# Two tiles of attention output go back to tokens together

## The chip, the cores and the metric

One core of one Trainium2 chip runs the whole program in one launch. The metric is device time in microseconds (us). Before the change three runs took 2543.44, 2546.03 and 2556.37 us; the median is 2546.03 us.

Five engines work side by side and each takes its instructions in the order in which they were built: TensorE (PE, its weight loads shown apart as PEld), VectorE (DVE), ScalarE (ACT), GpSimd (POOL) and SyncE (SP), which here only issues transfers. Results of PE land in PSUM, where this program has two kinds of tiles, banks of 512 columns and pairs of 1024.

## The reference, cut to what matters

Eight sequences of 256 tokens, 128 features each, pass through four blocks. Each block adds an attention to a given context and then an FFN, both behind a layer norm and both scaled by a gate:

```python
x = x + jnp.tanh(g_xattn[n]) * xattn_n(_layernorm(x), ctx_1024, ...)
x = x + jnp.tanh(g_ffn[n]) * ffn_n(_layernorm(x), ...)
```

The blocks differ. Block 0 has a linear attention, and its "FFN" is a self-attention of 16 heads of 8 features plus eight linear experts. Block 1 keeps the 64 largest scores of each row (8 heads of 64). Block 2 is a plain attention of 16 heads of 8, block 3 the same with the 32 largest scores of each row kept. Their output projection is

```python
qh, kh, vh = proj(q, Wq, bq), proj(k, Wk, bk), proj(v, Wv, bv)
attn = softmax(einsum('bhqd,bhkd->bhqk', qh, kh) / sqrt(8))
out = einsum('bhqk,bhkd->bhqd', attn, vh).transpose(0, 2, 1, 3).reshape(B, S, 128)
return einsum('bsd,ed->bse', out, Wo) + bo
```

The FFNs of blocks 1 to 3 are mixtures of 8, 8 and 16 experts; that of block 3 has the experts' projections around an attention of one head.

## The kernel before

**Tiling.** The 2048 tokens stay on the chip in four groups (`NG`), each a tile `xs[g]` of 128 partitions by 4 token tiles by 128 features. A group holds two batches (sequences, `bb`) of 256 tokens, so a batch is two token tiles, numbered `2 * bb + qc`.

**Way back of an attention output.** Attention with small heads leaves its output transposed: features of four heads, padded to 32 rows each, on the partitions, tokens along the columns, in two tiles `oTs` of a batch. `heads_back` (L336) turns it back. For each of the two token tiles it transposes four 128x128 pieces into a bank `pn` (L341), takes the reciprocals of the softmax sums, which lie in column 8 of each head (L345), multiplies and writes the 128 features of the tile to a tile `o_sb` of the ring `out2` (L347), and passes it to `done`. There are two sorts of `done`. Block 0's FFN adds the tile to the residual at once, with `add_gated` (L1081, L290). Blocks 2 and 3 run `out_proj` (L320): transpose `o_sb` into a bank `pt_o` (L324), copy it with ACT to `oT` (L326), multiply it by the output weights into a bank `po` (L330), add the bias by a further matmul (L333), and add the bank to the residual with `add_gated`. `out_proj` had an argument for several chunks of features, which is 1 in both uses. Block 1 has its own way back (L1229) and calls `add_gated` too.

Banks are a ring of 4, pairs a ring of 2, `out2` a ring of 6: a new tile waits until the tile that had its place is no longer used.

**Order of the work.** The program is written by Python generators, which yield between small steps. Two streams of them are interleaved by `side_by_side` (L72), by a time that each reports. One, `largest_scores` (L1683), holds the attentions of blocks 1 and 3, whose search for the largest scores is done on DVE with MAX8 and MATCH_REPLACE8 (`largest`, L385 and L389, block 3) or on ACT, POOL and DVE by counting (block 1). The other, `others` (L1799), holds all other stages, in the order of the list at L1793. A stage of one stream may start only when a set says that the other stream has got there: `finished` (called `largest_3` outside) gets a group in block 3's `finish` (L1394) after the group's last `heads_back`, and block 3's FFN of group `g` may start when `g` is in it, that of group 0 when group 2 is as well (L1763).

Behind a body, the rest of the stage before (`heads_back`, wrapped in `Ahead` with a number of steps: 6 in `attention_T.body`, 12 for block 3's `weigh` that ends in `finish`) is taken step by step as the body goes on. In the attentions with largest scores the unit is a chunk `k` of four heads: `units` searches chunk `k`, calls `fetch(k + 1)` for the next one's scores (L420, L427) when three of its four heads are through, and beside it the chunk before is weighed.

The generators only fix the order in which the program is written. Within it a scheduler of the framework, with a timeline of its own, orders the instructions of each engine.

Of the kernel before, what the change touches and what calls it, by code (L numbers as in the profile page):

```python
# [14 lines left out]
ALU = mybir.AluOpType  # L15
AX = mybir.AxisListType

P = 128
D = 128
B = 8  # L20
S = 256
# [69 lines left out]
def gated_blocks_kernel(ctx: ExitStack, tc: tile.TileContext, a, out):  # L91
    nc = tc.nc
# [8 lines left out]
    def program(exact):  # L101


        def cst(shape, name, dt=F32):
            return const.tile(shape, dt, tag=name, name=name)
# [4 lines left out]
        def bank(name="bank"):  # L110
            return psum.tile([P, 512], F32, tag="bank", name=name, bufs=4)
# [8 lines left out]
        def out2(name):  # L120
            return act.tile([P, 512], F32, tag="out2", name=name, bufs=6)
# [5 lines left out]
        xs = []  # L127
# [23 lines left out]
        ident = cst([P, P], "ident")  # L151
# [3 lines left out]
        biases = cst([P, D], "biases")  # L155
# [67 lines left out]
        tgx = cst([P, 4], "tgx")  # L223
        tgf = cst([P, 4], "tgf")
# [36 lines left out]
        def layer_norm(g):  # L261

            xg = xs[g]
            st = small.tile([P, NT, 6], F32, tag="st", name="st", bufs=2)
            mv = small.tile([P, NT, 2], F32, tag="mv", name="mv", bufs=2)
            for t in range(NT):
                nc.vector.bn_stats(st[:, t, :], xg[:, t, :])
                nc.vector.bn_aggr(mv[:, t, :], st[:, t, :])
            ve = small.tile([P, NT], F32, tag="ve", name="ve")
            nc.vector.tensor_scalar_add(ve, mv[:, :, 1], LN_EPS)  # L270
            rstd = small.tile([P, NT], F32, tag="rstd", name="rstd")
            nc.gpsimd.tensor_tensor(rstd, ve, neg_half[:, 0:NT], ALU.pow)
            xn = act.tile([P, NT, D], F32, tag="xn", name="xn", bufs=2)
            for t in range(NT):
                nc.vector.tensor_scalar(
                    xn[:, t, :], xg[:, t, :], mv[:, t, 0:1], rstd[:, t : t + 1], ALU.subtract, ALU.mult
                )
            yield
            yield
            pt = bank("pt_ln")  # L280
            for t in range(NT):
                nc.tensor.transpose(pt[:, t * P : (t + 1) * P], xn[:, t, :], ident)
            xnT = act.tile([P, W], F32, tag="xnT", name="xnT", bufs=3)
            nc.scalar.copy(xnT, pt)
            yield
            return xn, xnT

        def add_gated(g, t, src, gate):

            nc.vector.scalar_tensor_tensor(xs[g][:, t, :], src, gate, xs[g][:, t, :], ALU.mult, ALU.add)  # L290

        def heads_T(w, src, bias, scale, tag):

            dst = act.tile([P, 4, S], F32, tag=tag, name=tag, bufs=2)
            for cp in range(2):
                pp = bank("pp").rearrange("p (c q) -> p c q", c=2)
                for j in range(2):
                    c = 2 * cp + j
                    nc.tensor.matmul(pp[:, j, :], lhsT=w[:, c * P : (c + 1) * P], rhs=src, start=True, stop=True)  # L299
                if bias is None:  # L300
                    nc.scalar.mul(dst[:, 2 * cp : 2 * cp + 2, :], pp, scale)
                else:
                    for j in range(2):
                        c = 2 * cp + j
                        nc.scalar.activation(dst[:, c, :], pp[:, j, :], AF.Identity, bias=bias[:, c : c + 1], scale=scale)
            return dst

        def values16(w, srcT, width, tag):

            va = act.tile([P, 2, 16, width], F32, tag=tag, name="va", bufs=2)  # L310
            if width > 9:
                nc.gpsimd.memset(va[:, :, :, 8:width], 0.0)
            nc.gpsimd.memset(va[:, :, :, 8:9], 1.0)
            pp = bank("pv")[:, 0:256].rearrange("p (t d) -> p t d", t=2)
            for t in range(2):
                nc.tensor.matmul(pp[:, t, :], lhsT=srcT[:, t * P : (t + 1) * P], rhs=w, start=True, stop=True)
            nc.scalar.copy(va[:, :, :, 0:8], pp.rearrange("p t (h d) -> p t h d", d=8))
            return va

        def out_proj(g, t, o_sb, chunks, w, bias, gate):  # L320

            pt = bank("pt_o")
            for c in range(chunks):
                nc.tensor.transpose(pt[:, c * P : (c + 1) * P], o_sb[:, c * P : (c + 1) * P], ident)  # L324
            oT = out2("oT")
            nc.scalar.copy(oT[:, 0 : chunks * P], pt[:, 0 : chunks * P])  # L326
            yield
            po = bank("po")
            for c in range(chunks):
                nc.tensor.matmul(  # L330
                    po[:, 0:D], lhsT=oT[:, c * P : (c + 1) * P], rhs=w[:, c, :], start=(c == 0), stop=False
                )
            nc.tensor.matmul(po[:, 0:D], lhsT=bias, rhs=biases, start=False, stop=True)  # L333
            add_gated(g, t, po[:, 0:D], gate)

        def heads_back(g, bb, oTs, done):  # L336

            for qc in range(2):
                pn = bank("pn").rearrange("p (c r d) -> p c r d", c=4, r=4)
                for c in range(4):  # L340
                    nc.tensor.transpose(  # L341
                        pn[:, c].rearrange("p r d -> p (r d)"), oTs[c // 2][:, c % 2, qc * P : (qc + 1) * P], ident
                    )
                rec = small.tile([P, 4, 4], F32, tag="rec", name="rec")
                nc.vector.reciprocal(rec, pn[:, :, :, 8])  # L345
                o_sb = out2("o_sb")[:, 0:D].rearrange("p (c r d) -> p c r d", c=4, r=4)
                nc.vector.tensor_tensor(  # L347
                    o_sb, pn[:, :, :, 0:8], rec.unsqueeze(3).to_broadcast([P, 4, 4, 8]), ALU.mult
                )
                yield  # L350
                yield from done(g, 2 * bb + qc, o_sb.rearrange("p c r d -> p (c r d)"))

        def chunk_products(o, va, c, es):

# [312 lines left out]
        class attention_T:  # L667
# [5 lines left out]
            def __init__(self, g, prepare, done):  # L673
                self.g, self.prepare, self.done = g, prepare, done
# [71 lines left out]
            def body(self, first):  # L746

                behind = Ahead(0, iter(()))
                second = Ahead(11, self.ready(1))
                for bb, operands in ((0, first), (1, None)):  # L750
                    oTs = []
                    others = [behind]
                    if bb == 0:
                        others.append(second)
                    else:
                        operands = second.finish()
                    for f in alongside(self.weigh(*operands, oTs), *others):
                        yield (bb + f) / 2
                    behind = Ahead(6, heads_back(self.g, bb, oTs, self.done))
                return behind  # L760
# [118 lines left out]
        for g in range(NG):  # L879
            pt = bank("pt_c")  # L880
# [5 lines left out]
            for t in range(NT):  # L886
                n = g * NT + t
# [190 lines left out]

        class block0_ffn:
            def __init__(self, g):  # L1080
                def done(g, t, o):  # L1081
                    add_gated(g, t, o, tgf[:, 0:1])
                    yield

                self.g, self.att = g, attention_T(g, self.operands, done)
# [256 lines left out]
        def context_operands(n, weights, k=""):  # L1342
            wq, wk, wv, wo, bq, bk, bo = weights
            norms = {}

            def prepare(g, bb):
                if g not in norms:
                    norms[g] = yield from layer_norm(g)
                xnT = norms[g][1][:, bb * S : (bb + 1) * S]
                cT = ctxT[:, g * W + bb * S : g * W + (bb + 1) * S]  # L1350
                kT = heads_T(wk, cT, bk, 1.0, "kT" + k)
                yield
                qT = heads_T(wq, xnT, bq, INV_SQRT8, "qT" + k)
                yield
                return qT, kT, values16(wv, cT, 32, "va" + k)

            def done(g, t, o):
                yield from out_proj(g, t, o, 1, wo.unsqueeze(1), bo, tgx[:, n : n + 1])
                yield

            return prepare, done
# [6 lines left out]
        def block3_xattn(groups, weights, rounds, room, dropped, may_start, finished):  # L1368
# [25 lines left out]
            def finish(i, g, bb):  # L1394
                yield from heads_back(g, bb, oTs.pop(i), done)
                if bb == 1:
                    finished.add(g)
# [490 lines left out]
```

## Time and profile before

| what | value |
|---|---|
| median of three runs | 2546.03 us |
| the profiled execution | 2546.42 us, its span 2544.7 us |
| busy PE, PEld | 2123.7 us (83%), 1292.4 us (51%) |
| busy DVE, ACT, POOL | 1762.5 us (69%), 1149.0 us (45%), 879.8 us (35%) |
| granted TensorE clock, mean | 0.862 |
| MAX8 of block 3's search (L385) | 326.8 us, x768 from `wk`, 426 ns each |
| DMA | 13 GB/s in the mean |

The span reaches from the first to the last instruction. A busy share is an average over stages with different limits: block 1's search runs from about 150 to 1150 us, block 3's from 1192 to 2347 us, and block 3's FFN fills the rest to 2538 us. A row of a group shows line, engine, operation, output and input tile, shapes, count, then busy time and mean ns of one, then idle time before it with what ended most of it. A row of the timeline shows start, duration, engine, line, operation, and in brackets the idle time just before and its releaser.

### The profile page before, as it was taken

The page shows a single profiled execution, that of the slowest core. Times are in us where ns is not written, and L with a number is a line of the kernel's source. Part 1 is how long each engine was busy: PE and PEld are TensorE (multiplying, and loading weights), DVE is VectorE, ACT ScalarE, POOL GpSimd, SP SyncE. Part 2 cuts the span into 40 slices and gives each one's busy share as a digit, 9 for nine tenths or more (in the row PEclk, how much of TensorE's full clock was granted, in tenths as well). Part 3 has the DMA queues.
Part 4 walks back from the last instruction along what each step waited for, and adds up shares of the span by engine and source line. Part 5 has one row for each costly group of instructions (what it writes and reads, how often), then busy time and mean ns, then how long its engine had stood idle before and what let it go on. Part 6 is the DMA issues. An engine that isn't in the chain of part 4 may idle for free.

```text
span 2544.7 us, 35734 instructions
## 1 busy us (share of the span) xinstructions
PE 2123.7 (83%) x12068; PEld 1292.4 (51%) x12094; DVE 1762.5 (69%) x5463; ACT 1149.0 (45%) x2437; POOL 879.8 (35%) x2252
## 2 busy tenths in 40 slices
PE   7998888887878778888989868899676975988898
PEld 5655455554445444445444435445343444666677
DVE  4635757756765667665899879894798869798332
ACT  2236556546554677864355433464333542322101
POOL 3104434434432464531334324341233334233000
PEclk8999889978988889998599966899775986999999
DMA  2000001000000000010001100021000110000000
GB/s 63 6 1 2 1 1 32 1 1 1 1 1 1 1 26 1 26 34 22 1 1 42 34 1 1 1 59 50 1 1 1 42 42 1 1 5 1 5 5 6
DMA packets 47896, 32.97 MB, mean 13 GB/s; under 512 B 4747, under 2 KB 42838, under 8 KB 47702
## 3 DMA queue, kind: packets, MB, share of 16 engines
q1 hardware_dynamic: 47702, 30.58, 4.2%
q8 instruction: 97, 1.59, 0.3%
q14 instruction: 97, 0.79, 0.1%
HBM read 29.53 MB, written 1.05 MB: 12 GB/s over the span
## 4 chain that ended last, share of the span: by engine, by line
DVE 39%; PE 36%; ACT 13%; POOL 8%; issue 4%; DMA 0%; DVEq 0%; SPq 0%; ACTq 0%; POOLq 0%
DVE m L385 13%; DVE wk L389 12%; ACT signs L495 4%; PE sm L687 3%; PE sw L723 3%; PE ph L1476 3%; PE pp L299 3%; PE y L1445 2%; DVE nmz L695 2%; PE po L1635 2%; ACT sign L495 2%; PE oT L357 2%; PE o L1216 2%; DVE xe L851 2%; DVE list L542 1%
## 5 line engine op out<-in xcount | busy, mean ns | idle before, releaser
L392 POOL TENSOR_SCALAR mask<-rooms,m 128x256 bf16<-128x256 f32 x192 | 223.3, 1163 | 385.5 <-DVE m L385 353.4
L385 DVE MAX8 m<-wk 128x8 f32<-128x256 f32 x768 | 326.8, 426 | 37.0 <-DVE wk L389 0.9
L723 PE MATMUL sw<-qT,kT 32*128 32x256 f32 x1024 | 172.4, 476 | 68.3 <-ACT eK L599 24.1
L695 DVE TENSOR_REDUCE nmz<-sm 128x4 f32<-128x1024 f32 x128 | 154.9, 1219 | 105.1 <-PE sm L687 96.6
L389 DVE MATCH_REPLACE8 wk<-m,wk 128x256 f32<-128x256 f32 x512 | 208.9, 408 | 0.0
L495 ACT ACTIVATE signs<-room,nt 128x256 bf16<-128x256 f32 x288 | 145.9, 507 | 128.7 <-POOL nt L527 78.5
L687 PE MATMUL sm<-kT,qT 32*128 32x256 f32 x1024 | 152.6, 440 | 40.0 <-DVE nmz L695 28.4
L592 ACT ACTIVATE kept<-mask 128x1024 bf16<-128x1024 bf16 x64 | 67.6, 1057 | 227.3 <-POOL mask L392 227.1
L1476 PE MATMUL ph<-xnT,we 128*128 128x512 f32 x288 | 156.2, 638 | 15.5 <-ACT hT L1477 7.4
L723 PEld LDWEIGHTS sw<-qT,kT 32*128 32x128 f32 x1024 | 101.0, 222 | 128.4 <-DVE nmz L695 32.3
L737 ACT ACTIVATE eT<-sw 128x1024 f32<-128x1024 f32 x128 | 129.6, 1019 | 79.9 <-PE sw L723 73.9
L574 PE MATMUL sw<-qTk,kTk 32*128 32x256 f32 (+1 forms) x768 | 120.8, 456 | 53.6 <-DVE qTk L1383 35.2
L1445 PE MATMUL y<-hT,we 128*128 128x512 f32 x288 | 146.0, 620 | 0.6 <-DVE wb_sb L1457 0.6
L687 PEld LDWEIGHTS sm<-kT,qT 32*128 32x128 f32 x1024 | 92.3, 205 | 101.0 <-DVE nmz L695 42.9
L1477 ACT ACTIVATE hT<-ph,b 128x512 f32<-128x512 f32 x144 | 98.4, 686 | 98.8 <-PE ph L1476 94.4
L599 ACT ACTIVATE eK<-sw 128x1024 f32<-128x1024 f32 x96 | 96.6, 1019 | 89.4 <-PE sw L584 88.5
L420 PE MATMUL sp<-kTk,qTk 32*128 32x256 f32 (+1 forms) x768 | 121.1, 448 | 14.8 <-ACT eT L737 6.5
L357 PE MATMUL oT<-eT,va 128*32 128x256 f32 x1024 | 120.6, 449 | 10.2 <-ACT eT L737 9.3
L392 POOL TENSOR_SCALAR mask<-room,m 128x256 bf16<-128x256 f32 x64 | 74.5, 1164 | 155.2 <-DVE m L385 152.8
L574 PEld LDWEIGHTS sw<-qTk,kTk 32*128 32x128 f32 (+1 forms) x768 | 71.5, 212 | 96.1 <-issue 42.4
L420 PEld LDWEIGHTS sp<-kTk,qTk 32*128 32x128 f32 (+1 forms) x768 | 72.5, 209 | 59.5 <-issue 17.0
L387 POOL TENSOR_SCALAR nmk<-m 128x1 f32<-128x1 f32 x256 | 59.5, 232 | 100.7 <-DVE m L385 100.6
(381 smaller groups left out, 4976.2 us busy)
## 6 DMA issues: line engine op xcount, KB each, us to landing
we<-in_L_ffn_exp_w_dram SPq DMA_DIRECT2D x64, 256.0 KB
we<-in_L_ffn_shared_w_dram SPq DMA_DIRECT2D x8, 256.0 KB
x<-in_x_dram SPq DMA_DIRECT2D x4, 256.0 KB
big_ctx<-in_ctx_dram SPq DMA_DIRECT2D x4, 256.0 KB
w1f<-in_L_ffn_fc_w_dram SPq DMA_DIRECT2D x1, 1024.0 KB
w3a<-in_L_ffn_q_proj_dram SPq DMA_DIRECT2D x4, 256.0 KB
w3a<-in_L_ffn_k_proj_dram SPq DMA_DIRECT2D x4, 256.0 KB
w3b<-in_L_ffn_v_proj_dram SPq DMA_DIRECT2D x4, 256.0 KB
```

The lines of the kernel that those rows point to most:

```text
L357: nc.tensor.matmul(o[32 * r : 32 * r + 32, :], lhsT=va[:, n, 4 * c + r, :], rhs=es[r // 2][:, r % 2, n, :], start=(n == 0), stop=(n == 1),)
L385: nc.vector.max(m8, src[:, j, :])
L389: nc.vector.match_replace(wk[:, j, :], m8, src[:, j, :], LOWEST)
L392: nc.gpsimd.tensor_scalar(mask[:, j, :], s[:, j, :], m8[:, 7:8], 1.0, ALU.is_lt, ALU.mult)
L420: nc.tensor.matmul(sps[r // 2][:, r % 2, qc, :], lhsT=qT[rs, c, qc * P : (qc + 1) * P], rhs=kT[rs, c, :], start=(qc == 0), stop=(qc == 1),)
L495: nc.scalar.activation(to, s[:, j, :], AF.Sign, bias=nt[:, j : j + 1], accum_out=acc[:, j : j + 1])
L574: nc.tensor.matmul(sps[r // 2][:, r % 2, m, :], lhsT=kT[rs, c, m * P : (m + 1) * P], rhs=qT[rs, c, :], start=(m == 0), stop=False,)
L687: nc.tensor.matmul(sps[r // 2][:, r % 2, j, :], lhsT=qT[rs, 2 * cp + j, qc * P : (qc + 1) * P], rhs=kT[rs, 2 * cp + j, :], start=(j == 0), ...
L695: nc.vector.tensor_reduce(nmz[:, qc, 2 * cp : 2 * cp + 2, 2 * h : 2 * h + 2, 8].rearrange("p c r -> p r c"), sps[h], AX.X, ALU.max, negate ...
L723: nc.tensor.matmul(sps[r // 2][:, r % 2, n, :], lhsT=kT[rs, c, n * P : (n + 1) * P], rhs=qT[rs, c, :], start=(n == 0), stop=(n == 1),)
L1445: nc.tensor.matmul(y, lhsT=w2[:, c, :], rhs=hs[c // 2][:, js], start=(c == 0), stop=(c == 3))
L1476: nc.tensor.matmul(pp[:, js], lhsT=w1[:, c * P : (c + 1) * P], rhs=xnT, start=True, stop=True)
```

## The change

`heads_back` now takes one `o_sb` of 256 columns for a batch, writes both token tiles into it, and calls `done` once, with the batch's number, after one more yield. `out_proj` transposes both tiles into one bank, copies 256 columns at once, multiplies both into one bank `po` (each tile's product and its bias one after the other), and adds 256 columns at once. `add_gated` takes either one tile or, with a source of three dimensions, the two tiles of a batch. Block 0's FFN adds its two tiles at once. Numbers of transposes and matmuls are as before; block 1 is as before.

```diff
--- before.py
+++ after.py
@@ -287,7 +287,8 @@
 
         def add_gated(g, t, src, gate):
 
-            nc.vector.scalar_tensor_tensor(xs[g][:, t, :], src, gate, xs[g][:, t, :], ALU.mult, ALU.add)
+            x = xs[g][:, 2 * t : 2 * t + 2, :] if len(src.shape) == 3 else xs[g][:, t, :]
+            nc.vector.scalar_tensor_tensor(x, src, gate, x, ALU.mult, ALU.add)
 
         def heads_T(w, src, bias, scale, tag):
 
@@ -317,24 +318,23 @@
             nc.scalar.copy(va[:, :, :, 0:8], pp.rearrange("p t (h d) -> p t h d", d=8))
             return va
 
-        def out_proj(g, t, o_sb, chunks, w, bias, gate):
+        def out_proj(g, bb, o_sb, w, gate, bias):
 
             pt = bank("pt_o")
-            for c in range(chunks):
-                nc.tensor.transpose(pt[:, c * P : (c + 1) * P], o_sb[:, c * P : (c + 1) * P], ident)
-            oT = out2("oT")
-            nc.scalar.copy(oT[:, 0 : chunks * P], pt[:, 0 : chunks * P])
+            for qc in range(2):
+                nc.tensor.transpose(pt[:, qc * P : (qc + 1) * P], o_sb[:, qc * P : (qc + 1) * P], ident)
+            oT = out2("oT")[:, 0:S]
+            nc.scalar.copy(oT, pt[:, 0:S])
             yield
-            po = bank("po")
-            for c in range(chunks):
-                nc.tensor.matmul(
-                    po[:, 0:D], lhsT=oT[:, c * P : (c + 1) * P], rhs=w[:, c, :], start=(c == 0), stop=False
-                )
-            nc.tensor.matmul(po[:, 0:D], lhsT=bias, rhs=biases, start=False, stop=True)
-            add_gated(g, t, po[:, 0:D], gate)
+            po = bank("po")[:, 0:S].rearrange("p (t d) -> p t d", t=2)
+            for qc in range(2):
+                nc.tensor.matmul(po[:, qc, :], lhsT=oT[:, qc * P : (qc + 1) * P], rhs=w, start=True, stop=False)
+                nc.tensor.matmul(po[:, qc, :], lhsT=bias, rhs=biases, start=False, stop=True)
+            add_gated(g, bb, po, gate)
 
         def heads_back(g, bb, oTs, done):
 
+            o_sb = out2("o_sb")[:, 0:S]
             for qc in range(2):
                 pn = bank("pn").rearrange("p (c r d) -> p c r d", c=4, r=4)
                 for c in range(4):
@@ -343,12 +343,13 @@
                     )
                 rec = small.tile([P, 4, 4], F32, tag="rec", name="rec")
                 nc.vector.reciprocal(rec, pn[:, :, :, 8])
-                o_sb = out2("o_sb")[:, 0:D].rearrange("p (c r d) -> p c r d", c=4, r=4)
                 nc.vector.tensor_tensor(
-                    o_sb, pn[:, :, :, 0:8], rec.unsqueeze(3).to_broadcast([P, 4, 4, 8]), ALU.mult
+                    o_sb[:, qc * P : (qc + 1) * P].rearrange("p (c r d) -> p c r d", c=4, r=4), pn[:, :, :, 0:8],
+                    rec.unsqueeze(3).to_broadcast([P, 4, 4, 8]), ALU.mult,
                 )
                 yield
-                yield from done(g, 2 * bb + qc, o_sb.rearrange("p c r d -> p (c r d)"))
+            yield
+            yield from done(g, bb, o_sb)
 
         def chunk_products(o, va, c, es):
 
@@ -1078,8 +1079,8 @@
 
         class block0_ffn:
             def __init__(self, g):
-                def done(g, t, o):
-                    add_gated(g, t, o, tgf[:, 0:1])
+                def done(g, bb, o):
+                    add_gated(g, bb, o.rearrange("p (t d) -> p t d", t=2), tgf[:, 0:1])
                     yield
 
                 self.g, self.att = g, attention_T(g, self.operands, done)
@@ -1354,8 +1355,8 @@
                 yield
                 return qT, kT, values16(wv, cT, 32, "va" + k)
 
-            def done(g, t, o):
-                yield from out_proj(g, t, o, 1, wo.unsqueeze(1), bo, tgx[:, n : n + 1])
+            def done(g, bb, o):
+                yield from out_proj(g, bb, o, wo, tgx[:, n : n + 1], bo)
                 yield
 
             return prepare, done
```

## The prediction

> **What bounds the kernel now.** I read the page's chain of waits first, then the busy time by stretches, then the touched instructions with their waits, and last the timeline around the batches concerned.
>
> ```profile
> DVE 39%; PE 36%; ACT 13%; POOL 8%; issue 4%; DMA 0%; DVEq 0%; SPq 0%; ACTq 0%; POOLq 0%
> ```
>
> No engine owns the chain that ended last, so the stretches decide. These are us, then the busy time of PE, PEld, DVE, ACT and POOL, then the granted TensorE clock:
>
> ```profile
> 850.00:1150.00 300.00, 244.11 (x1305) 133.25 (x1309) 199.72 (x615) 206.72 (x515) 145.74 (x516) 0.93 0.06 19
> 1150.00:1350.00 200.00, 177.47 (x918) 96.28 (x921) 157.84 (x548) 91.45 (x136) 64.03 (x105) 0.81 0.03 8
> 1850.00:2160.00 310.00, 226.06 (x1070) 127.43 (x1071) 255.94 (x895) 115.80 (x195) 120.46 (x175) 0.75 0.06 18
> 2380.00:2545.00 165.00, 146.32 (x722) 123.17 (x720) 46.95 (x83) 16.68 (x47) 3.57 (x9) 0.93 0.02 4
> ```
>
> DVE sets the pace from about 1150 to 2350 us, where it finds block 3's largest scores (L385, L389). PE alone sets the last 165 us. Summing the chain by stretch: DVE has 782 of the 1530 us between 850 and 2380, PE 407; in 0 to 850 DVE has 199.
>
> The touched instructions are small. By group, and by tile, with minimum/median/maximum ns:
>
> ```profile
> L290 DVE SCALAR_TENSOR_TENSOR x<-po,tgx,x 128x128 f32<-128x128 f32 x48 | 16.2, 343 | 14.5 <-PE po L1237 7.3 <-PE po L333 7.1
> L290 DVE SCALAR_TENSOR_TENSOR x<-o_sb,tgf,x 128x128 f32<-128x128 f32 x16 | 5.4, 342 | 0.3
> L869 DVE SCALAR_TENSOR_TENSOR x<-pt_y,tgf,x 128x256 f32<-128x256 f32 x8 | 3.8, 479 | 5.6 <-PE pt_y L867 5.6
> L326 ACT COPY oT<-pt_o x32: 243/265/285, 907.3 to 2378.8; 128x128 f32<-128x128 f32 x32
> L1639 ACT COPY yT<-po x8: 353/372/378, 2187.7 to 2537.6; 128x256 f32<-128x256 f32 x8
> ```
>
> L869 and L1639 are the same operations at 256 columns. On the chain, the lines L290 (all callers), L324, L326, L330, L333, L345 and L347 have only 24 of 2545 us.
>
> A batch on its way back, on PE, and DVE some 50 us later:
>
> ```profile
> 2106.39 0.47 PE L324 MATMUL pt_o<-ident,o_sb 128*128 128x128 f32 x1 [4.09 <-DVE o_sb L347]
> 2107.22 0.80 PE L330 MATMUL po<-wo,oT 128*128 128x128 f32 x2 [0.35 <-ACT oT L326]
> 2107.81 0.63 PE L333 MATMUL po<-biases,ident 128*128 128x128 f32 x2
> 2110.66 0.45 PE L324 MATMUL pt_o<-ident,o_sb 128*128 128x128 f32 x1 [1.36 <-DVE o_sb L347]
> ...
> 2160.47 0.69 DVE L1603 TENSOR_REDUCE nm<-s 128x2 f32<-128x512 f32 x1 [1.70 <-PE s L1593]
> 2162.60 0.42 DVE L1383 TENSOR_TENSOR qTk<-qTk,pt_mk 128x256 f32<-128x256 f32 x1 [1.44 <-PE pt_mk L1382]
> 2168.43 0.17 DVE L1621 RECIPROCAL rec<-o 128x2 f32<-128x2 f32 x1 [5.41 <-PE o L1617]
> ```
>
> In brackets stands the idle time before an instruction. PE stands still for DVE twice, once for each tile, and for ACT's copy after each. DVE has no idle time there: it is the one that is late.
>
> **Part by part.** *Additions.* Block 0's 16 additions of 0.342 us become 8; blocks 2 and 3's 32 of 0.343 become 16 (the other 16 of the x48 belong to block 1's L1238 and stay). At 0.479 that is 5.47 - 3.83 = 1.64 and 10.98 - 7.66 = 3.31 us less on DVE. No row has the 256-column form with an SBUF source; at 128 columns the two sources cost the same (342 and 343), so I take 0.479 for it, between no gain over two additions (0.684) and one 128-column addition (0.342), which moves the sum by at most 1.6 us either way. Weighed by DVE's share of the chain (199/850 and 782/1530): 0.4 + 1.7 = -2.1 us.
>
> *Copies.* 32 x 0.265 - 16 x 0.372 = 2.5 us of ACT; at its 13% of the chain -0.3. The rest lies beside DVE's search; without that cover it is 2.5.
>
> *Matmuls.* As many transposes (32), products (64 rows of L330) and bias rows (64 of L333) as before, so nothing.
>
> *Waits.* PE's idle time before L324 for L347 is 33.0 us in 13 places. Four are a first tile's, 8.18, 6.74, 5.33 and 4.09 us (at 1525, 1839, 1948 and 2106): DVE is behind, and now both tiles' transposes wait for two reciprocals and two multiplications instead of one each, so these stay and grow by L345 and L347 (0.25 + 0.28). The second tiles' waits, 1.16 + 1.36 + 1.75 + 1.36 + 0.42 = 6.1, fall away, and half of the 7.3 us for ACT's copies (L330). PE gets back 6.1 + 3.6 - 4 x 0.5 = 7.7 us; at PE's 407 of 1530, -2.0. What is late next in these places is DVE, which gains nothing from an earlier PE. Behind the joint wait stand, in PE's queue, the four products and four bias rows of this batch, and behind them the next unit's shift and scores; they come sooner (before, 5.7 us lay between the first and the last addition's matmuls of the batch at 2106; now one round trip).
>
> At this point a rule speaks against the change. The trace's first addition (2108.48) ran while PE already worked in other banks. The Trainium skill, PSUM — Partial Sum Buffer, "PSUM bank collisions raise a hardware error", says that two engines may not be in one bank and quadrant at once, so tile 1's addition out of a shared bank has to wait for tile 2's matmuls. By the rule alone 16 batches times 1.2 us (2107.22 to 2108.44, the four rows of a tile) would be +19 us. The trace shows nobody who needs the first tile alone: the layer norm takes all four tiles of a group. By the rows it is nothing.
>
> *What moves.* `out_proj` now yields once for a batch, so `heads_back` ends after 5 yields, not 6, inside block 3's `weigh` after 8, not 9, of 12 steps. Block 3's FFN of group 0 may start when group 2 is in `finished`; it is now written before the next unit's `fetch`, not behind it. The order in the built programs shows this as the one far move on PE: the fetch's eight matmuls (L420, begun at 2093.7 and 2097.5, 2.1 us each half) now stand behind the third of that FFN's four groups of projections (groups at 2134.9, 2142.9, 2148.5 and 2153.7). The other order hardly changes, and landmarks on DVE keep their distance less the removed additions. The price: DVE's search now runs dry. Between the FFN's first and third `xe` (L851) 8 rows or so are left for it, at 0.46 us (MAX8 0.43, MATCH_REPLACE8 with its load 0.50). The third and fourth wait for PE (9.5 and 15 us behind the first, as before), idle 3.4 + 4.3; then the third group, the fetch (2.2 us at the full clock) and its copy (L427, 1.0), idle some 7; with two waits of 2 us more, 18.7. On the other side DVE's old idle time, from 2158.8 to 2180.7, 1.70 + 1.44 + 5.41 + 2.78 + 2.50 + 2.38 = 16.2 us, is filled by the search rows held back. Net +2.5, between -16 (all filled, and the new gap covered) and +14.7 (3.4 + 4.3 + 7 opened, old idle time kept). I take +2, near the balance, as the same rows stand on both sides.
>
> Sum: -2.1 - 0.3 - 2.0 + 2 = -2.4. The profiled execution took 2546.4 (span 2544.7 and 1.7 around it), the median is 2546.0: **2543.5**, say 2543.
>
> A second rule bears on the stalls. Where PE had idled for 4 to 8 us the trace shows it slow: the granted clock is 0.50 in 2100 to 2130 and L330 takes 0.58 us where it takes 0.38 or less elsewhere. The skill's TensorE: Matmul & The Clock Gate, Part 1, says that an idle window of about 3.4 us halves the clock and about as much work restores it. By the rule the 1 to 2 us stalls that go away don't change the clock, and the 4 to 8 us ones that stay still halve it; by the rows the same, with nothing for the sum.
>
> **The rivals.** *A, faster: the shorter way back counts in full.* If PE's released time (7.7) and all DVE (4.95) and ACT (2.5) savings are on the path, that is -15, and the gap behind 2158.8 filled could add up to -16: 2531, in a band of 2520 to 2533. For it: after each such stall PE has a queue full of work, and block 2's products feed DVE (L695 waits 96.6 us for PE). Against it: DVE is 92% busy between 2180 and 2347 and without a gap over 1 us from 1846 to 1966.
>
> *B, slower: the late fetch.* The new idle time (18.7) comes in full and the old one (16.2) stays, because the FFN's attention (L1603 to L1621, 8 us of PE and ACT round trips) stays as long and search rows don't fall into it. Then the search, which is the path up to 2347, ends that much later, PE waits in order for its masks, and PE's 2.0 is worth nothing beside it: 2546.4 - 2.4 + 18.7 = 2563, in a band of 2559 to 2567. It decides once more than some 15 us of new idle time reach the end. For it: the search goes straight to the end of the stretch. Against: the rows fill the gap in the built order, 19 of them between L1603 and L1621.
>
> *C, nothing of it.* The additions' columns cost as much as two, the order's moves balance: 2546. It falls into the forecast's class.
>
> **How the numbers follow.** Forecast with C 0.48, A 0.28, B 0.24. I give A and B more than their arguments alone, since local exchanges of a few rows on all engines follow from the change and I priced one of them. 0.5%, 13 us, is about what a measurement of this kernel can tell from no change; so within 2533 to 2559 stands 0.48, faster 0.28, slower 0.24. The range is 2525 to 2562: it takes in the upper 8 of the 13 us of A's band and the lower 3 of the 8 of B's, which leaves out some 2 in 10. The forecast's own range is 2534 to 2555.
>
> **What would show it.** Right: L290's row with 24 additions of 128x256 at about 480 ns, L326's with 16 copies at about 370; PE's idle time before the transposes near 25 us, in half as many places; DVE's idle time after 2158 halved and a new one of 10 to 17 us between 2135 and 2155; the search ending within 8 us of 2347. Wrong: a stage away from these, such as 850 to 1150 where ACT and POOL set the pace, that differs by more than 8 us; DVE's idle time up by more than 17; an addition above 600 ns.

## The result, and the profile after

The changed kernel took 2560.4 us (median of 8 runs, 2551.8 to 2562.4), the kernel before 2547.8 in the same comparison (8 runs, 2543.4 to 2556.4): a ratio of 1.0034, 95% interval 1.0018 to 1.0051. By this ratio it is 8.7 us slower (4.6 to 13.0), where 2.4 us faster had been forecast; the two medians alone lie 12.6 us apart. The profiled execution took 2552.6, with a span of 2550.9 against 2544.7.

The page of the changed kernel: span, busy time of the engines, and the engines' shares of the chain that ended last.

```profile
span 2550.9 us, 35706 instructions
PE 2141.1 (84%) x12067; PEld 1303.4 (51%) x12094; DVE 1754.8 (69%) x5439; ACT 1147.3 (45%) x2421; POOL 882.2 (35%) x2252
DVE 38%; PE 37%; ACT 13%; POOL 7%; issue 5%; DMA 0%; DVEq 0%; SPq 0%; ACTq 0%
```

DVE was busy for 1762.5 us before: 7.7 less now. PE was busy for 2123.7 before, with one instruction more in the trace: 17.4 more now, for the same work. PE's idle time fell by 11.2 (421.0 to 409.8, span less busy time); the sum of the two, +6.2, is the longer span. So the change did save waiting, and TensorE became slower at its work.

Where this happens is seen when matching instructions of both traces (on DVE, ACT and POOL) are laid beside each other: the changed kernel is 6.9 us late at 600 us, 23.9 at 850, 28.0 at 1150, 12.1 at 2100 and 6.2 at the end. Stretches whose ends lie within 2 us of the same instructions, first before, then after (us; busy time and count of PE, PEld, DVE, ACT, POOL; clock, DMA):

```profile
600.00:850.00 250.00, 207.24 (x1230) 120.82 (x1231) 165.66 (x458) 142.53 (x363) 97.35 (x355) 0.88 0.00 1
850.00:1150.00 300.00, 244.11 (x1305) 133.25 (x1309) 199.72 (x615) 206.72 (x515) 145.74 (x516) 0.93 0.06 19
1150.00:2100.00 950.00, 790.75 (x3936) 421.41 (x3946) 763.23 (x2513) 419.06 (x640) 332.93 (x491) 0.81 0.07 20
2100.00:2544.70 444.70, 367.52 (x2073) 293.59 (x2073) 275.69 (x816) 86.86 (x182) 86.77 (x143) 0.90 0.01 3
```

```profile
606.70:875.50 268.80, 225.50 (x1234) 130.53 (x1236) 166.09 (x457) 146.75 (x369) 98.75 (x359) 0.80 0.00 1
875.50:1177.00 301.50, 248.45 (x1302) 134.74 (x1301) 197.82 (x612) 205.91 (x509) 144.33 (x511) 0.90 0.06 18
1177.00:2113.00 936.00, 780.55 (x3925) 418.83 (x3936) 762.28 (x2505) 414.26 (x629) 332.87 (x491) 0.82 0.07 20
2113.00:2550.90 437.90, 364.71 (x2086) 292.19 (x2086) 273.94 (x811) 85.58 (x176) 86.91 (x143) 0.92 0.01 3
```

The stretch from 600 us grew by 18.8 (17.0 from instruction to instruction), PE's busy time in it by 18.3 with 1234 instructions for 1230, at a clock of 0.80 for 0.88. PE's idle time in it is nearly the same (42.8 and 43.3 us), so this loss is TensorE's slower clock. Here block 0's feed-forward ends and block 1's search runs; of the touched code only block 0's way back lies in it. The two stretches that hold most of blocks 2 and 3 became 14.0 and 6.8 us shorter. Of the 14.0, 10.2 are PE's busy time, at a clock of 0.82 for 0.81, and 3.8 its idle time. The touched rows of the changed kernel, by tile and by group:

```profile
L291 DVE SCALAR_TENSOR_TENSOR x<-o_sb,tgf,x x8: 464/485/505, 181.1 to 866.2; 128x256 f32<-128x256 f32 x8
L327 ACT COPY oT<-pt_o x16: 351/373/395, 945.4 to 2386.5; 128x256 f32<-128x256 f32 x16
L291 DVE SCALAR_TENSOR_TENSOR x<-po,tgx,x 128x128 f32<-128x128 f32 (+1 forms) x32 | 12.9, 408 | 16.2 <-PE po L1238 13.0 <-PE po L332 2.8
L325 PE MATMUL pt_o<-ident,o_sb 128*128 128x128 f32 x32 | 8.4, 333 | 23.5 <-DVE o_sb L346 23.4
```

### The profile page after: what moved, and what is told of

Read it like the earlier page. It is cut to its first block, busy times and chain, and to the rows that moved or that the text cites. A ratio compares the mean times of both kernels' runs of the same rounds, so it can differ in the third digit from the quotient of the medians.

```text
span 2550.9 us, 35706 instructions
## 1 busy us (share of the span) xinstructions
PE 2141.1 (84%) x12067; PEld 1303.4 (51%) x12094; DVE 1754.8 (69%) x5439; ACT 1147.3 (45%) x2421; POOL 882.2 (35%) x2252
## 4 chain that ended last, share of the span: by engine, by line
DVE 38%; PE 37%; ACT 13%; POOL 7%; issue 5%; DMA 0%; DVEq 0%; SPq 0%; ACTq 0%
DVE m L386 13%; DVE wk L390 12%; ACT signs L496 5%; PE sm L688 3%; PE sw L724 3%; PE pp L300 3%; PE ph L1477 2%; DVE nmz L696 2%; PE o L1217 2%; ACT sign L496 2%; PE y L1446 2%; PE oT L358 2%; PE po L1636 2%; DVE xe L852 2%; PE pqk L1581 1%
## 5 line engine op out<-in xcount | busy, mean ns | idle before, releaser
L575 PE MATMUL sw<-qTk,kTk 32*128 32x256 f32 (+1 forms) x768 | 129.7, 482 | 57.1 <-DVE qTk L1384 37.4
```

Source lines behind the costliest of these rows:

```text
L575: nc.tensor.matmul(sps[r // 2][:, r % 2, m, :], lhsT=kT[rs, c, m * P : (m + 1) * P], rhs=qT[rs, c, :], start=(m == 0), stop=False,)
```

## Experiments

Ratios are to the kernel before on the same chip, with 95% intervals. Medians of the kernel before differ by chip (2547.8 to 2560.7 us), so times of different groups are not compared.

**First group: which part.** `block0_only` has the change in block 0 alone: `heads_back` twice, the new one for block 0, the old one for the others.

```
-                self.g, self.att = g, attention_T(g, self.operands, done)
+                self.g, self.att = g, attention_T(g, self.operands, done, heads_back_0)
```

> Blocks 2 and 3 as before, block 0's feed-forward with the joint store and one addition of 256 columns for both tiles. Theory 1 (the loss is block 0's own: its first tile is now added a step and a half later, and the changed kernel's profile was some 24 us behind by 850 us, before any code of blocks 2 and 3 runs for its later half): slower than before by 8 us or more, 2556 to 2568, and a profile again 15 to 25 us behind at 850 us. Theory 2 (the fetch moved behind finished in block 3): 2547, nothing. Theory 3 (the edit only permutes the order and with it the stretches in which TensorE runs at half clock): anything from 2538 to 2558, and the part that is behind coincides with more half-clock time.

Measured: 1.0071 (1.0054 to 1.0089), and the profile 20 us behind at 850 us. From 150 to 860 us the changed kernel keeps a distance of 2.7 to 2.9 us to `block0_only`, so all that it loses there is block 0's. `blocks23_only` is its mirror, with the old `heads_back` and the two additions for block 0 and the new way back for blocks 2 and 3:

> Block 0 as before, blocks 2 and 3 changed in full. Theory 1: faster than before, since the changed kernel won some 18 us back between 1150 and 2160 us: about 2530 to 2538. Theory 2: as slow as the changed kernel, 2556 to 2562. Theory 3: anything from 2538 to 2558.

Measured: 0.9892 (0.9871 to 0.9912), 2531.7 us: it beats both kernels, and up to 850 us its profile lies within 0.3 us of the kernel before. Theory 1 holds for both in kind, but the gain here, 28 us by the ratio, is above the 10 to 18 that it gave. `six_steps` is the whole change with one more step:

```
             def done(g, bb, o):
+                yield
                 yield from out_proj(g, bb, o, wo, tgx[:, n : n + 1], bo)
```

> The whole change, with one empty step more on the way back of blocks 2 and 3, so that it has six steps again and the fetch of the next unit comes before finished as before the change. Theory 1: as slow as the changed kernel, 2556 to 2562. Theory 2: back to the forecast, 2541 to 2548. Theory 3: anything from 2545 to 2565.

Measured: 0.9963 (0.9946 to 0.9980), as the sum of the two parts (+0.71 and -1.08%). By the ratio that is 2538 us where the kernel before took 2547.8, below the ranges of all three theories: still 22 us behind at 850, more won back later. `block0_order` merges nothing and only writes block 0 in the new order:

```
+            parts = []
             for qc in range(2):
...
                 yield
-                yield from done(g, 2 * bb + qc, o_sb...)
+                parts.append(o_sb...)
+            yield
+            yield from done(g, bb, parts)       # two additions of 128 columns
```

> The kernel before, with block 0's two additions of 128 columns written together in the place where the change has its single one; two stores, two additions. Theory 1 with the late addition as its cause: as block0_only. Theory 1 with the shared store or the longer addition as its cause: 2547. Theory 3: anything from 2538 to 2558.

Measured: 1.0072 (1.0045 to 1.0099), as `block0_only`. So the order alone costs as much, without the shared store and the wide addition. But it pays elsewhere: its profile is 17 us behind at 600 us already (`block0_only` 4; some 8 of it may be chance, see `before_again`) and 22 at 850.

**Second group: which step of block 0's order.** The change writes the second tile's transposes, reciprocal and multiplication at the second step, where the kernel before had them at the third, and the first tile's addition at the fourth, not the second. `block0_gap` puts the tile back and leaves the addition late; `block0_early` leaves the tile early and takes the addition forward to it, with the two empty steps behind.

```
             for qc in range(2):
+                if qc:
+                    yield            # block0_gap: second tile at its old step
```

> Blocks 2 and 3 as before; block 0 with the shared store and the one addition, but its second tile's transposes are written at their old step (the third), an empty step in between; only the first tile's addition is later than before. If the later first addition costs (theory L): as block0_only, 1.005 to 1.009 of before. If it is the second tile's four transposes and reciprocal, which the change writes one step sooner (theory E): back to 0.998 to 1.002. If any small shift early in the program changes the half-clock stretches behind it (theory 3): anywhere from 0.994 to 1.009.

Measured: 1.0030 (1.0014 to 1.0047), its runs from 2543 to 2575 us; its profile, that of the fastest of the 12 runs, is 3.4 us ahead of the first one of before at 700 to 850, not behind.

> Blocks 2 and 3 as before; block 0 with the shared store, the second tile one step sooner as in the change and the addition right behind it, two steps before its place in the change; as many steps in all. Theory L (first addition later by one step only, and the second one sooner by two): 0.998 to 1.003. Theory E: as block0_only, 1.005 to 1.009. Theory 3: anywhere from 0.994 to 1.009.

Measured: 1.0092 (1.0071 to 1.0112). So it is mostly the early tile; the late addition and what else moves leave 0.3%. The profiles say it more sharply. The three of the changed kernel, `block0_only`, `block0_early` and `six_steps` all fall back by a further 16 to 17 us between 600 and 850 us, with 123 of the 300 us from 600 to 900 at half clock. All kernels without the early tile and without added products (those below included) fall back by 0 to 7, with 78 to 105 at half clock. `block0_order`, with the tile early and everything unmerged, lies between: 5 us and 104.

What the early tile does is seen on PE in block 1's feed-forward of group 2. First the kernel before, then the changed one (start and duration in us; `wb` spreads the routing weights that DVE waits for):

```profile
612.29 0.60 PE L341 MATMUL pn<-ident,oT 128*128 128x128 f32 x4
...
613.62 0.38 PE L839 MATMUL wb<-w_parts,spread 128*128 128x512 bf16 x1
...
618.13 0.60 PE L341 MATMUL pn<-ident,oT 128*128 128x128 f32 x4
618.57 0.38 PE L839 MATMUL wb<-w_parts,spread 128*128 128x512 bf16 x1
```

```profile
618.71 0.60 PE L341 MATMUL pn<-ident,oT 128*128 128x128 f32 x4
...
620.04 0.60 PE L341 MATMUL pn<-ident,oT 128*128 128x128 f32 x4
...
623.91 0.38 PE L840 MATMUL wb<-w_parts,spread 128*128 128x512 bf16 x1
...
635.06 1.13 PE L421 MATMUL sp<-kTk,qTk 64*128 64x256 f32 x8 [1.74 <-ACT eK L600]
637.93 1.97 PE L1217 MATMUL o<-eK,va 128*64 128x256 f32 x8 [1.74 <-ACT xnT L284]
```

Four transposes came forward by one place, and the `wb` product that had stood between the tiles comes 5.2 us behind the first tile's transposes, not 1.3. Some 10 us later PE stands still twice for 1.74 us, and from the end of the second stall on everything takes double: L1217's eight products 1.97 us, where they took 1.08. The clock explains that: cut into the 3.41 us steps in which it is granted, the changed kernel shows (columns as above)

```profile
629.86:633.28 3.42, 3.42 (x25) 2.20 (x23) 3.42 (x14) 2.39 (x7) 0.66 (x4) 1.00 0.02 5
633.28:636.69 3.41, 1.17 (x9) 0.69 (x8) 1.18 (x4) 3.37 (x4) 0.00 (x0) 1.00 0.00 0
636.69:640.10 3.41, 2.17 (x10) 1.23 (x12) 3.08 (x12) 2.59 (x6) 2.35 (x9) 0.50 0.02 5
640.10:643.52 3.42, 3.42 (x11) 1.41 (x8) 3.42 (x10) 1.80 (x6) 1.11 (x6) 0.50 0.00 0
```

In one step PE was busy for 1.17 of 3.41 us (the first stall and 0.50 us of the second lie in it), and the next two ran at half clock. At the same place the least busy step of the kernel before had 2.30 of 3.41, and it kept its clock from 603.5 to 682.0.

This place is an example and not the most of the loss, and that the late `wb` makes the stalls was not tried. `block0_gap`, with `wb` at its old place, also stands still there, for 2.22 us, and loses its clock for one step. The place costs 6 of the 17 us (3 in `block0_gap`). Some 12 are lost between 760 and 815 us, behind a stall of 7.15 us: from 756.2 to 793.7 us the clock was half, 37.5 us, where the kernel before needed 20.5 behind the like stall.

`before_again` and `after_again` are the two kernels themselves, for the size of chance.

> The kernel before, unchanged, under another name: measures what these comparisons can tell. All theories: 0.998 to 1.002, and a second profile whose raster of 3.41 us steps of the granted clock lies elsewhere against the program. If the phase of that raster decides the loss in 600 to 860 us, this profile shows 100 us or more at half clock there (first profile of before: 78 in 600 to 900); if the order of the instructions decides it, 65 to 90.

Measured: 0.9996 (0.9984 to 1.0009). The steps of the clock lay 2.07 us earlier against the program; the profile fell 8 us behind at 150 us, regained 9.7 between 1150 and 1600 and lost 7 near 2330, and kept its distance to the first within 0.3 us from 200 to 850. In 600 to 900 us 80.2 us were at half clock, 78.5 the first time (122.8 in `block0_only`): there the order decides, not the phase with which an execution starts.

> The changed kernel, unchanged: 1.002 to 1.005 again, on the chip of the other runs of this group, so that the parts can be added up. By the parts (block 0 alone +0.7%, blocks 2 and 3 alone -1.1%) it should be 0.996; if it is 1.003 again, the parts do not add up, and the fetch behind finished (theory 2) or the shift of blocks 2 and 3 against the raster is worth the rest, 0.7%.

Measured: 1.0016 (1.0001 to 1.0031). The parts don't add up exactly: their sum is 0.996.

**Third group: what gains in blocks 2 and 3, and the repair.** All four on one chip. `blocks23_six` is `blocks23_only` with the `yield` of `six_steps`.

> Block 0 as before; blocks 2 and 3 changed, with an empty step so that the way back has six steps and the fetch comes before finished as in the kernel before. If the moved fetch costs by itself (theory 2): faster than the changed blocks 2 and 3 with five steps (0.989 of before), 0.980 to 0.985. If the fetch is worth nothing: 0.987 to 0.991. If the gain of those blocks comes from the order and not from the merged operations: anywhere from 0.987 to 1.003, with the difference to 0.989 in TensorE's time at half clock.

Measured: 0.9943 (0.9924 to 0.9962): putting the fetch back gains nothing there. `blocks23_two_adds`:

```
-            add_gated(g, bb, po, gate)
+            for qc in range(2):
+                add_gated(g, 2 * bb + qc, po[:, qc, :], gate)
```

> Block 0 as before; blocks 2 and 3 with shared banks and one copy, but two additions of 128 columns out of the shared bank. If the wider addition is worth what the rows say (3.3 us of VectorE, half of it on the path): 0.990, no difference that can be told from 0.989. If the additions are what gains: 0.995 or more.

Measured: 0.9966 (0.9952 to 0.9980), outside of what the rows allow for. `blocks23_order` keeps a bank, a copy and an addition for each tile:

```
+            for qc in range(2):
+                pt = bank("pt_o")
+                nc.tensor.transpose(pt[:, 0:P], parts[qc], ident)
...
+            yield
+            for qc in range(2):
+                po = bank("po")[:, 0:D]
...
+                add_gated(g, 2 * bb + qc, po, gate)
```

> Block 0 as before; in blocks 2 and 3 nothing is merged (two stores, two banks, two copies, two additions), only written in the new order: both tiles' stores, then both transposes and copies, then both products and additions. If the gain is the order's (fewer places in which TensorE waits for VectorE, less half clock): 0.988 to 0.993. If it is that of the merged operations or of the banks saved (four instead of six for a batch): 0.997 to 1.003.

Measured: 0.9918 (0.9900 to 0.9937), the lowest of these three although it merges nothing: an order alone gives a gain of that size there. What merging gives is not shown by it, since four versions that differ by little stand between 0.989 and 0.997. `all_gap` is the whole change with the `yield` of `block0_gap`:

> The whole change, only that block 0's second tile keeps its old step. If the loss is that step's alone: 0.989 to 0.994, 1% under the changed kernel. If block 0's half and the other two simply do not add up because each shifts the other: 0.994 to 1.003.

Measured: 0.9849 (0.9816 to 0.9881), 2508.6 us, below every expectation: one empty step is worth 1.4 to 1.9% of the changed kernel. By the profiles it gains 25 us on the changed kernel between 200 and 900 us, where the step works, and 19 behind 900, where nothing was edited.

**Fourth group: is half clock the cause?** `block0_filled` adds work that nobody reads to `block0_only`, where its longest stretch at half clock of the first 1500 us began. To have a place for it, the score products of that batch are also written in another order:

```
+ # group 3, second batch, in front of the last four score products
+ spare = bank("spare")
+ for _ in range(12):
+     nc.tensor.matmul(spare[0:64, :], lhsT=nmz[...], rhs=wq0, start=True, stop=True)
```

> block0_only with twelve products of 64x512 that nobody reads, in one place: group 3 of block 0, in front of the last four score products of its second batch, where TensorE stood still for 7.2 us for VectorE's maximum at 755 to 762 us and the longest stretch at half clock (37.6 us) began. If that stretch is what costs (cause): the clock stays whole or the stretch shrinks to 14 us or less, the 40 us behind the place take 10 to 18 us less than in block0_only, and the kernel 1.001 to 1.005 of before instead of 1.007 to 1.009, although it has 5 us more work. If the half clock only goes with the loss: the 40 us behind take as long as before or longer, 1.007 to 1.011.

First `block0_only` without it, in steps of the clock, then both kernels' PE from the timeline, the second with the added products:

```profile
753.50:756.91 3.41, 1.21 (x8) 0.40 (x4) 0.00 (x0) 2.44 (x10) 1.23 (x8) 0.50 0.00 0
756.91:770.57 13.66, 6.16 (x24) 3.54 (x24) 11.25 (x32) 7.54 (x25) 6.69 (x27) 0.50 0.00 1
...
773.98:791.05 17.07, 17.07 (x63) 9.82 (x62) 3.83 (x4) 3.07 (x6) 0.89 (x2) 0.50 0.00 1
791.05:794.46 3.41, 3.41 (x22) 2.34 (x21) 0.00 (x0) 2.38 (x4) 0.00 (x0) 1.00 0.00 0
```

```profile
761.89 2.08 PE L707 MATMUL sm<-kT,qT 32*128 32x256 f32 x8 [7.19 <-DVE nmz L715]
...
793.07 1.94 PE L1190 MATMUL pv<-wkv,ctxT 128*128 128x512 f32 x4
```

```profile
759.59 2.08 PE L711 MATMUL sm<-kT,qT 32*128 32x256 f32 x8 [5.41 <-ACT eT L761]
763.29 2.07 PE L711 MATMUL sm<-kT,qT 32*128 32x256 f32 x8 [1.62 <-DVE nmz L719]
765.29 11.81 PE L709 MATMUL spare<-w,nmz 128*64 128x512 f32 x24
777.03 1.13 PE L711 MATMUL sm<-kT,qT 32*128 32x256 f32 x8
...
796.21 1.94 PE L1194 MATMUL pv<-wkv,ctxT 128*128 128x512 f32 x4
```

The stall came ahead of the added products (5.41 and 1.62 us), so they did not fill it, but behind it the clock was whole again after 10.2 us, not 37.6. From the last score products to the values' product it took 19.2 us, not 31.2; 2.5 of the 12.0 are waits for DVE that the added products now cover. The kernel, 4.3 us later than `block0_only` before the place, was 3.1 later at the values' product and level with it at 850 (0.3 to 0.8 us ahead on PE), with 11.8 us of useless work done, where 5 had been reckoned. That this work cost nothing fits a clock that was whole. It points to half clock as the cause there, though the other order of the score products was not tried alone. The 40 us behind the place were to take 10 to 18 us less; they took 1 to 5 less. For the whole kernel the expectation failed: 1.0103 (1.0083 to 1.0123); it loses again after 1250 us.

`all_gap_filled` has the same lines in `all_gap`:

> The same twelve idle products in the best version so far (the whole change with block 0's second tile at its old step). There the stretch behind the stall was shorter (20 us in the kernel before), so if the clock is the cause: 4 to 10 us less behind the place, 0.981 to 0.985 of before. If not: 0.985 to 0.988.

Measured: 0.9980 (0.9964 to 0.9996), 40 us above the version without it. Only 3 us were gained at the place. The rest was lost between 850 and 2000 us, most of it behind 1400, where DVE's order differs in dozens of places although nothing was edited there: presumably the scheduler carries a shift in its own time forward.

`all_order` joins `blocks23_order` with block 0's order of `all_gap`, two stores and two additions:

> Nothing merged: two stores, two banks, two copies, two additions everywhere, but written in the order of the best version (blocks 2 and 3 both tiles together; block 0 second tile at its old step, both additions at the end). If the gain is the order's alone: 0.984 to 0.990. If the merged operations are worth what the rows say (VectorE 5 us, ScalarE 2.5 us, weighed 2.4): 0.001 above all_gap_again. If they make the gain: 0.995 to 1.003.

Measured: 0.9914 (0.9888 to 0.9940); `all_gap_again` on the same chip:

> The best version again, for its interval beside the other three: 0.982 to 0.989 if its gain holds on another chip; 0.994 or more if the first time was luck.

Measured: 0.9822 (0.9798 to 0.9846), 2512.4 us. Its gain repeats. Without merging 24 us of it are missing, ten times the 2.4 that the rows give for the merged operations, while in blocks 2 and 3 alone the unmerged version was no slower. As each variant is also ordered anew, these runs do not separate the two.

**Last group: the fetch again.** `all_gap_six` is `all_gap` with the `yield` of `six_steps`, `after_third` the changed kernel.

> The best version with six steps on the way back of blocks 2 and 3, so that the fetch of the next unit comes before finished as in the kernel before. If the moved fetch costs (theory 2; putting it back gained 0.6% in the whole change): 0.974 to 0.979 of before. If it is worth nothing by itself: 0.980 to 0.987. If that gain came only from where the order falls: up to 0.993.

Measured: 0.9921 (0.9905 to 0.9938). Here putting the fetch back costs, in `six_steps` it gained. It has no price of its own that shows.

> The changed kernel on the chip of the run above: 1.001 to 1.005 of before by its two earlier comparisons, 1.6 to 2.3% above the version with block 0's step put back.

Measured: 0.9989 (0.9976 to 1.0002). On three chips the changed kernel stands at 1.0034, 1.0016 and 0.9989: about no change, and always far above the repaired version. The three intervals hardly meet, so they hold less than all of the chance between chips.

## Why the prediction was wrong

*Additions: right.* 485 ns measured for 479 taken, with a source in SBUF; the joint ones of blocks 2 and 3 up to 486. *Copies: right*, 16 of 373 ns.

*Waits: right in kind and size.* PE's idle time before the transposes for DVE fell from 33.0 to 23.4 us, in four places for four batches (8.67, 6.12, 6.58, 2.06); about 25 had been forecast. The stretch of 1150 to 2100 gained 14.0, not some 4, but only 3.8 of that is PE's idle time; the other 10.2 is busy time, which the forecast took as fixed.

*Tile 1's addition out of the shared bank: by the rows.* The Trainium skill, PSUM — Partial Sum Buffer, "PSUM bank collisions raise a hardware error", would have made the first tile's addition wait for the second tile's products. DVE's idle time before these additions was 2.8 us in all (7.1 before), not 19 more. The one addition for both tiles waits for both tiles' products anyway, so this does not try the rule itself.

*The moved fetch: mechanism right, sign wrong.* The new idle time of DVE came, and the old one went:

```profile
2146.04 1.22 DVE L852 TENSOR_TENSOR xe<-xnT,wb 128x1024 f32<-128x1024 f32 x1 [3.07 <-PE wb L840]
2151.66 1.22 DVE L852 TENSOR_TENSOR xe<-xnT,wb 128x1024 f32<-128x1024 f32 x1 [4.40 <-PE wb L840]
2159.03 0.43 DVE L386 MAX8 m<-room 128x8 f32<-128x256 f32 x1 [6.15 <-ACT room L428]
```

That is 13.0 us idle in 2135 to 2158 (10 to 17 were named), and from 2158.8 to 2190 only 2.1, where 16.2 had been. Matching search instructions were 13.3 us late at 2123 and 9.3 at 2181: -4.0, not +2. Rival B is out. That the search still ended 9.9 us late (8 had been named) was lost before.

*The step that failed* is "Additions. Block 0's 16 additions of 0.342 us become 8", priced at -0.4, together with "What moves", which looked only where the number of steps changed. In block 0 that number stays at four, but what stands in them moved: the second tile from the third step to the second. The diff's `heads_back` says so in three lines, and no part of the sum priced it. In `block0_only` it costs 0.7%, some 18 us. None of the three rivals holds it. The sentence "a stage away from these ... that differs by more than 8 us" comes near: 600 to 850, where block 0's way back ends, differs by 18.8. Nor did the sum see the gain of blocks 2 and 3: -2.0 us in it (-1.7 - 0.3 - 2.0 + 2), 28 us by `blocks23_only`. The whole stays near the kernel before because two effects that the forecast did not have work against each other; that the third comparison (0.9989) comes out at the forecast's 2.4 us or so is luck.

*The clock term failed with it.* By the prediction "the 1 to 2 us stalls that go away don't change the clock", and the sum has nothing for it. At 636.7 two stalls of 1.74 us, of which 2.24 us in all lay in one step, halved it. The Trainium skill's TensorE: Matmul & The Clock Gate, Part 1, speaks of an idle window of about 3.4 us; the traces agree on the length of the window, but it need not be idle: 1.17 us of work in it did not hold the clock.

What stays open: why the parts do not add up (0.996 by the parts, 0.999 to 1.003 measured; 0.992 by `block0_gap` and `blocks23_only`, 0.982 to 0.985 measured). Up to 850 us the parts do add up, as the profiles of `block0_only` and `blocks23_only` show, so the rest arises behind that. That a small edit reorders the built program hundreds of microseconds away is shown; how much of each difference comes from that was not tried apart. Also open is by which chain of waits the early tile brings the clock down.

## What to carry to other kernels

Ask of every step of a generator whether what stands in it moved, also where the number of steps is the same: four transposes written one step sooner cost more than all merged operations were worth by the rows. Look at TensorE's busy time per instruction, not only at its idle time: when the first rises with the same count of instructions, the clock is the place to look; here short stalls close together within one step were enough to halve it. In a kernel whose scheduler carries every shift forward, compare variants by the trace up to the edit and just behind it, and take differences of the size seen here (12 idle products changed the whole by 1.6%) as order until a profile says otherwise.

## What was not expected of the hardware

The granted clock moves in steps of 3.413 us on a raster that ran on through each execution at a phase of its own (six first profiles: 0.7 to 2.7 us). In the ten profiles up to `after_again` all 344 steps at full clock in which PE was busy for under 40% were followed by half clock, and 37 of some 4060 in which it was busy for over 80%. The way back is less sharp: all 597 stretches at half clock that ended within the program ended with a step busy for over 80%, but 605 other steps busy for over 90% did not end theirs. In `block0_only` PE worked for 17.07 us without a gap at half clock, while in the kernel before, behind the like stall (7.72 us) and with the same products queued, the first full step sufficed:

```profile
743.40:746.81 3.41, 0.00 (x0) 0.00 (x0) 0.96 (x1) 3.38 (x14) 1.13 (x2) 0.50 0.00 0
746.81:760.47 13.66, 6.34 (x28) 3.65 (x32) 10.29 (x32) 7.45 (x24) 6.73 (x29) 0.50 0.00 1
760.47:763.88 3.41, 3.41 (x24) 1.56 (x24) 0.00 (x0) 2.94 (x7) 1.10 (x4) 0.50 0.00 0
763.88:767.29 3.41, 3.41 (x32) 1.93 (x30) 2.55 (x3) 0.00 (x0) 0.00 (x0) 1.00 0.02 5
```

Up to there the products behind the stall come in the same order in both; what differs is where the steps lie. In the six profiles named above with 123 us at half clock PE restarts 1.6 us into a step, although their rasters start at phases of 0.6 to 2.6 us. In the eleven of the kernels without the early tile and without added products it restarts 0.1 to 0.6 us into a step, from phases of 0.6 to 3.4 us, and the clock is back after 20 to 24 us, not 37.5. So an order of instructions falls into its own place against the raster, whatever the phase at the start, and this fits that the loss repeats. Which products fill the first full step (20 of L357 here) may matter; no run settles what the way back asks for.
